# An edge-gated graph layer on one core: the term beta1 h comes from the transposed h by TensorE in blocks 0 to 9, and for half of each later block

## The chip, the cores and the metric

The kernel runs on one core of a Trainium2 chip. The metric is the device time of one execution in microseconds. Before the change the median of three runs is 1077.57 us (1075.32 to 1079.38).

## What is computed

The input x has 16 graphs (b) of 1024 nodes (u, v) with 256 features (d); the adjacency adj is 1024 x 1024 and sparse. Cut to what matters, with A = adj:

```python
pre_u = einsum('bud,dk->buk', h, W1[:256])
pre_v = einsum('bvd,dk->bvk', h, W1[256:])
hidden = relu(pre_u[:, :, None, :] + pre_v[:, None, :, :] + b1)
S = sigmoid(einsum('buvk,ko->buvo', hidden, W2)[..., 0] + b2[0])
a = einsum('buv,bud->bvd', S * A, h)
m = einsum('uv,bud->bvd', A, h) * h
z = beta1 * h + beta2 * (a @ Wa + ba) + beta3 * (m @ Wm + bm)
```

The change concerns the first term of the last line, beta1 * h. All of it is in fp32.

## The kernel before, in words

**Blocks and steps.** A block is a group g of 4 graphs and a tile vt of 128 target nodes v; there are 4 x 8 = 32 blocks (`order`, L409). A block has T = 10 steps: two windows of 64 targets, five tiles of 128 edges each. The loop at L882 runs over n, the 320 steps and a few more; k is the block and s the step in it. In a step, GpSimd gathers 128 rows of a table in DRAM, [pre_u | h] of the source nodes for four graphs (`fetch`, L515, eight buffers `fetched`). TensorE spreads pre_v to the edges (`expand`, L610, into PSUM tile pc), VectorE adds pc to the gathered rows (`add`, L646) and makes the scores by relu, product with W2 and sum (`gate`, L650, four L656). ScalarE takes the sigmoid and builds the left operands (L625, L659, L661). TensorE sums the rows of h into the targets (`aggregate`, L664).

**A window's end and a block's end.** `half_end` (L678) copies the sums out, `turn_over` (L683) transposes them by TensorE (L691) into LT, and `times_h` (L702) multiplies the m half by the transposed h, hT. `block_end` (L710) is a generator that is run for block k - 1 in the steps z to z + 3 of block k, one quarter in each, with z = 4 from n = 10 on. It works in two halves h of two graphs. For each, TensorE puts the bias into PSUM (L719, L449) and adds the products with Wa and Wm (L722), eight matmuls of 256 columns. Then beta1 h is added to it:

- In every block but those of the last group's second half, ScalarE copies the PSUM tile to LT (L736), and one step later VectorE computes h beta1 + z in the tile h_blk (L737). Two steps later the store is issued on SP's queue (L739).
- In the second half of the blocks of the last group (24 to 30), TensorE adds be1_eye times h_blk (L726, two matmuls of 256 columns; be1_eye is the identity times beta1), ScalarE copies PSUM to h_blk (L728), and L730 stores it.

Block 31 has an ending of its own (`tail`, L753).

**Loads of h and of hT.** h_blk, 256 KB for a half, has four buffers and is loaded from the table on SP's queue in steps 5 and 7 of its own block (L916 to L922). hT, 512 KB for a block, is loaded by `load_hT` (L428), on SP's queue but for one; it is read by `rows` (L452, pre_u of a coming group, with w_u), by `halves` (L473, pre_v of the next block, with w_v) and by `times_h`, which after its last use gives the buffer back (`drop_hT`, L706). When hT is loaded and when `rows` uses it is a table written out by hand: `plan` (L787 to L798) gives for each tile the step of the load and of its two pieces. In groups 2 and 3 the load stands at first - 4 + 10 i and the pieces at first + 8 + 10 i and first + 12 + 10 i.

**The order on the engines** is the order in which the program issues (a manual schedule); `after(step, f)` puts f at the end of a later step. In steps up to 110 VectorE, TensorE and GpSimd also make the edge lists (`lists`, L242), in pieces that `fill` (L640) puts between the four L656 of a step. One of their tiles is few (L330), an 8-bit copy that GpSimd writes and four DMAs read. be1_eye is made at step 110 (L942); the other scalings with beta are made in `scale_late` (L599), at step 10.

Of the kernel before, what the change touches and what calls it, by code (L numbers as in the profile page):

```python
# [7 lines left out]
FP = mybir.dt.float32  # L8
# [3 lines left out]
ALU = mybir.AluOpType  # L12
AX = mybir.AxisListType
P = 128
# [3 lines left out]
def kernel(  # L18
# [42 lines left out]
    nc = tc.nc  # L61
    B, N, D = x.shape
    NT = N // P
    DC = D // P
    GB = 4
    NG = B // GB
    GD = GB * D
    W = 64
    NW = P // W
    TW = 5  # L70
    E = TW * P
# [170 lines left out]
    def lists(vt):  # L242
# [84 lines left out]
        nc.vector.tensor_tensor(thr[:, vt:vt + 1], last, none, ALU.add)  # L327
        yield "op"
        RR = lst.tile([P, NW, RC], FP, name="RR", bufs=2)
        few = lst.tile([P, E], mybir.dt.uint8, name="few", bufs=2)  # L330
        yield "slot"
        for w, mine in enumerate((soon, late)):
            nc.vector.tensor_scalar(RR[:, w, :], R, mine, None, ALU.mult)
# [68 lines left out]
    def after(step, f):  # L402
        due.setdefault(step, []).append(f)
# [19 lines left out]
    def drop_hT(k):  # L423
        del hTs[k]
        if k in hT_of:
            hT_free.append(hT_of.pop(k))
# [77 lines left out]
            pass  # L504

    T = TW * NW

    BS = NG * NT

# [89 lines left out]
    def scale_late():  # L599
        nc.vector.tensor_scalar(ba_b, ba_b, be2, None, ALU.mult)  # L600
        nc.vector.scalar_tensor_tensor(bias, bias, be3, ba_b, ALU.mult, ALU.add)
        spread(bias_p, bias)
        nc.vector.tensor_scalar(w_a, w_a, be2, None, ALU.mult)
        nc.vector.tensor_scalar(w_m, w_m, be3, None, ALU.mult)
        hT_free.append(spare_)

# [19 lines left out]

    running = []
    be1_eye = []  # L630

    def piece_of(r, n):

# [49 lines left out]
    def turn_over(k, w, q, step):  # L683
        if w == 0 and q == 0:
            LTs[k] = one.tile([P, GB, 2, DC, P], FP, name="LT")
        LT = LTs[k]
        pt = small("pt").rearrange("p (r k c v) -> p r k c v", r=2, c=DC, v=V)
        ev = evs.pop(q)
        for i in range(4):
            r, c = divmod(i, DC)  # L690
            nc.tensor.transpose(pt[:, r, :, c, :], ev[:, r, c * P:(c + 1) * P], ident)  # L691
        v = slice(w * W + q * U, w * W + (q + 1) * U)
        r = (w * W + q * U) // V
        nc.scalar.copy(LT.rearrange("p b k c (r v) -> p r (b k c) v", v=V)[:, r:r + 2],
                       pt.rearrange("p r k c v -> p r (k c) v"))
        apart = k == BS - 1 and w == NW - 1
        if not apart:
            if not q:
                return
            v = slice(w * W, (w + 1) * W)  # L700

        def times_h():  # L702
            m = LT.rearrange("p (b two) k c n -> p b (two k c) n", two=2)[:, :, DC:3 * DC, v]
            h = hTs[order[k]].rearrange("p (b two) c n -> p b (two c) n", two=2)[:, :, :, v]
            nc.vector.tensor_tensor(m, m, h, ALU.mult)  # L705
            if w == NW - 1 and q == 1:  # L706
                drop_hT(order[k])
        after(step + (1 if k == BS - 1 or w else 2), times_h)

    def block_end(k):  # L710

        g, vt = order[k]
        hb = hbs[k]
        for h in range(2):
            for i, wt in ((1, w_a), (0, w_m)):
                step = yield
                if i:
                    pz = small("pz")
                    add_row(pz, bias_p)  # L719
                for bb in range(2):  # L720
                    for c in range(DC):
                        nc.tensor.matmul(pz[:, bb * D:(bb + 1) * D], LTs[k][:, 2 * h + bb, i if bb else 1 - i, c, :], wt[:, c, :],  # L722
                                         start=False, stop=(i == 0 and c == DC - 1), skip_group_check=True)
            if h == 1 and g == NG - 1:
                for bb in range(2):
                    nc.tensor.matmul(pz[:, bb * D:(bb + 1) * D], be1_eye[0], hb[h][:, bb, :], start=False, stop=True,  # L726
                                     skip_group_check=True)
                nc.scalar.copy(hb[h], pz.rearrange("p (b d) -> p b d", b=2))  # L728
                b = g * GB + 2 * h
                after(step + 2, lambda hb=hb[h], b=b: nc.sync.dma_start(  # L730
                    out[b:b + 2, vt * P:(vt + 1) * P, :].rearrange("b p d -> p b d"), hb))
                continue
            z = pz.rearrange("p (b d) -> p b d", b=2)
            if step >= ROOM:
                z = LTs[k][:, 2 * h].rearrange("p k c n -> p (k c n)").rearrange("p (b d) -> p b d", b=2)
                nc.scalar.copy(z, pz.rearrange("p (b d) -> p b d", b=2))  # L736
            after(step + 1, lambda hb=hb[h], z=z: nc.vector.scalar_tensor_tensor(hb, hb, be1, z, ALU.mult, ALU.add))  # L737
            b = g * GB + 2 * h
            after(step + 2, lambda hb=hb[h], b=b: nc.sync.dma_start(  # L739
                out[b:b + 2, vt * P:(vt + 1) * P, :].rearrange("b p d -> p b d"), hb))  # L740
        del hbs[k], LTs[k]

# [42 lines left out]
    def plan(blocks, ns):  # L787

        for k, (load, *pieces) in zip(blocks, ns):
            loads[load] = k  # L790
            at.update((n, k) for n in pieces)

    plan(turn[NT:], ((1, 2, 4), (2, 8, 9), (5, 12, 18), (10, 19, 22), (20, 28, 29), (23, 32, 38), (30, 39, 42), (40, 48, 49)))
    for g, first in ((2, 60), (3, 140)):
        plan([(g, vt) for vt in range(NT)], ((first - 4 + 10 * i, first + 8 + 10 * i, first + 12 + 10 * i)
                                             for i in range(NT)))
    plan([(1, vt) for vt in range(FIRST)], [(37 + 10 * i,) for i in range(FIRST)])
    plan([(g, vt) for g in range(2) for vt in range(FIRST, NT)], ((103,), (113,), (125,), (133,)))  # L798
    begun = set(turn[:NT])
    end = parts = piece = last = None  # L800
# [81 lines left out]
    for n in range(total + 2):  # L882
        k, s = divmod(n, T)
        if n < total - 3:
            last_in = n - 1 if n % 2 or n < ROOM else done
        else:
            last_in = n
        while done < min(last_in, total):
            gather_in(done)
            done += 1  # L890
        if n % TW == 1 and n // TW + 1 < total // TW:
            load_mark(n // TW + 1)
        if n < LAST:
            expand(n + 2)
            if n >= ROOM:
                fill(n, False)
            products(n, k, s)
        if n + 1 < total:
            add(n + 1)
        if n < total:  # L900
            gate(n)
            if n + 1 < total:
                left_adj(n + 1)
        do(n)
        if s == 8 and ROOM <= n < LAST:
            turn_over(k, 0, 0, n)
        if n >= LAST and n + 2 < total:
            expand(n + 2)
        if n == 1:
            bias = load_rows(bm, D, "bias", nc.sync, spare[:, 1])  # L910
            ba_b = load_rows(ba, D, "ba_b", nc.sync, spare[:, 2])
            be1 = load_rows(beta1, 1, "be1", nc.sync)
            be2 = load_rows(beta2, 1, "be2", nc.sync)
            be3 = load_rows(beta3, 1, "be3", nc.sync)
            after(10, scale_late)
        if s in (5, 7) and k < BS - 1:  # L916
            h = s // 7
            hb = big.tile([P, 2, D], FP, name="h_blk", bufs=4)
            hbs.setdefault(k, []).append(hb)
            g, vt = order[k]  # L920
            nc.sync.dma_start(hb.rearrange("p b d -> p (b d)"),
                              table[g][vt * P:(vt + 1) * P, GD + 2 * h * D:GD + (2 * h + 2) * D])  # L922
        if n == total - 6:
            hbs[BS - 1] = hT_free.pop(0).rearrange("p b c n -> p b (c n)")
            for v, m, f in tails:
                for h, o in tail_rows(x, v, m, f):
                    nc.sync.dma_start(h, o)
        for i in advance.get(n, ()):
            next(made[i], None)
        if n in start_list:  # L930
            running.append([made[start_list[n]], True, n])
            piece_of(running[-1], n)
        if n < ROOM or n >= LAST:
            fill(n, False)
        if n >= LAST:
            products(n, k, s)
        if n == LISTS:
            assert not running and all(next(x, None) is None for x in made)
            lists_done()
            more = main.enter_context(tc.tile_pool(name="more", bufs=1))  # L940
            hT_free.extend(hT_places(more, MORE, NH))
            be1_eye.append(more.tile([P, P], FP, name="be1_eye"))  # L942
            nc.vector.tensor_scalar(be1_eye[0], ident, be1, None, ALU.mult)
        if n == 120:
            nc.gpsimd.partition_all_reduce(longest, rest, P, bass_isa.ReduceOp.max)
            after(n + 12, count_rest)
# [115 lines left out]
```

## Time and profile before

| what | value |
|---|---|
| median of 3 runs | 1077.57 us |
| the profiled execution | 1082.24 us, its span 1080.4 us |
| mean granted TensorE clock | 0.99 |
| DMA | 394.56 MB, mean 365 GB/s |
| gathers (queue 0) | 301.16 MB, 70.9% of the 16 engines' span |
| queue 1 (SP's loads and stores) | 78.66 MB, 22.9% |
| h_blk loads | 62 of 256 KB |
| stores of z from h_blk | 62 of 256 KB |

A page of the profile tells one execution: busy time by engine, the span in 40 slices, the DMA queues, the chain of work that ended last, and the costliest groups of instructions. PE is TensorE, PEld its weight loads, DVE VectorE, ACT ScalarE, POOL GpSimd, SP the engine that only issues DMAs. A group's line gives line number, engine, operation, what it writes and reads (out<-in), its shape and count, busy us and mean ns of one, and the idle time of the engine just before it with what ended it. An fp32 matmul stands in the trace as two records, and the ends of matmuls are modelled, so starts tell more than durations.

### The profile page before, as it was taken

The numbers are of one execution on the slowest core, as the hardware profiler recorded it, in microseconds if no ns is written. First come the engines' busy times: TensorE is split into PE (matmuls) and PEld (weight loads), VectorE is DVE, ScalarE is ACT, GpSimd is POOL, SyncE is SP. The second block draws the span as 40 slices with busy tenths as digits, with TensorE's granted clock in tenths as the row PEclk, the third lists the DMA queues.
The fourth block names the chain that finished last, engine by engine and source line by source line (L and its number), as shares of the span: only waits on it lengthen the run. The fifth ranks groups of instructions, "written<-read, shape, count | busy, mean of one in ns | idle before, by whom it ended". The sixth has DMA issues, their size and how long they took to land.

```text
span 1080.4 us, 24120 instructions
## 1 busy us (share of the span) xinstructions
PE 1020.1 (94%) x7673; PEld 731.3 (68%) x7673; DVE 1017.6 (94%) x3481; ACT 862.6 (80%) x2616; POOL 459.3 (43%) x456
## 2 busy tenths in 40 slices
PE   7777999999999999999999999999999999999996
PEld 6654676776666776677777767777766667666654
DVE  8687999998999999999999999999999999999993
ACT  3246787788888887898888888889889889999983
POOL 2666676555257334553333334333333333333330
PEclk9989999999999999999999999999999999999999
DMA  9999899999999999999999999999999999999991
GB/s 283 327 340 385 313 339 381 362 382 378 403 352 371 408 381 385 379 403 395 404 393 399 412 384 392 408 396 389 381 361 370 369 348 368 365 381 369 365 341 44
DMA packets 147752, 394.56 MB, mean 365 GB/s; under 512 B 18224, under 2 KB 94512, under 8 KB 111408
## 3 DMA queue, kind: packets, MB, share of 16 engines
q0 software_dynamic: 50544, 301.16, 70.9%
q1 hardware_dynamic: 83776, 78.66, 22.9%
q10 hardware_dynamic: 13296, 13.11, 3.5%
q8 instruction: 63, 1.03, 0.4%
q14 instruction: 73, 0.60, 0.1%
HBM read 396.93 MB, written 50.33 MB: 414 GB/s over the span
## 4 chain that ended last, share of the span: by engine, by line
PE 40%; DVE 34%; issue 10%; ACT 8%; DMA 5%; POOL 2%; another core or an unknown queue 0%; POOLq 0%; DVEq 0%; ACTq 0%
DVE fetched L656 16%; DVE fetched L648 12%; PE acc L673 10%; PE misc L722 10%; PE misc L445 9%; PE pc L615 7%; DMA fetched<-table,uidx 3%; PE misc L691 2%; ACT left L661 2%; DVE LT L705 1%; ACT X L489 1%; PE misc L449 1%; DVE low L484 1%; DVE h_blk L737 1%; DMA hT__635<-in_xT_dram 1%
## 5 line engine op out<-in xcount | busy, mean ns | idle before, releaser
L518 POOL DMA_INDIRECT fetched<-table,uidx x320 | 339.4, 1061 | 529.0 <-PE acc L673 389.0
L656 DVE SCALAR_TENSOR_TENSOR fetched<-fetched,w_b 128x256 f32<-128x256 f32 x1280 | 478.0, 419 | 0.0
L648 DVE TENSOR_TENSOR fetched<-fetched,pc 128x1024 f32<-128x1024 f32 x320 | 387.7, 1212 | 29.9 <-PE pc L615 19.4
L661 ACT ACTIVATE left<-left,gt 128x32 f32<-128x32 f32 (+1 forms) x1280 | 299.6, 305 | 10.4
L673 PE MATMUL acc<-fetched,left 128*32 128x256 f32 x4096 | 273.4, 385 | 6.3 <-ACT gt L659 3.7
L615 PE MATMUL pc<-X,mark 128*128 128x512 f32 x640 | 243.7, 462 | 10.9 <-DVE fetched L648 9.3
L673 PEld LDWEIGHTS acc<-fetched,left 128*32 128x32 f32 x4096 | 127.6, 109 | 112.1 <-issue 29.1
L615 PEld LDWEIGHTS pc<-X,mark 128*128 128x128 f32 x640 | 105.4, 189 | 88.9 <-issue 41.6
L659 ACT ACTIVATE gt<-sc,b_b 128x4 f32<-128x4 f32 x320 | 95.9, 300 | 46.7 <-DVE fetched L656 37.5
L722 PE MATMUL misc<-w_m,LT 128*128 128x256 f32 x496 | 117.3, 379 | 0.0
L722 PE MATMUL misc<-w_a,LT 128*128 128x256 f32 x496 | 117.2, 379 | 0.0
L445 PE MATMUL misc<-w_v,hT 128*128 128x256 f32 x448 | 107.6, 383 | 0.0
L722 PEld LDWEIGHTS misc<-w_a,LT 128*128 128x128 f32 x496 | 93.8, 189 | 15.3 <-issue 0.4
L722 PEld LDWEIGHTS misc<-w_m,LT 128*128 128x128 f32 x496 | 93.8, 190 | 15.1
L625 ACT ACTIVATE left<-onehot,val 128x64 f32<-128x64 bf16 (+1 forms) x320 | 102.9, 322 | 0.0
L385 POOL DMA_INDIRECT val<-in_adjT_dram,vidx x80 | 87.2, 1090 | 34.4 <-issue 20.4
L656 DVE DVE_READ_ACCUMULATOR fetched<-fetched,w_b 128x1 f32 x1280 | 100.7, 79 | 0.0
L691 PE MATMUL misc<-ident,ev 128*128 128x128 f32 x512 | 79.5, 278 | 18.5 <-issue 7.0
L445 PEld LDWEIGHTS misc<-w_v,hT 128*128 128x128 f32 x448 | 86.4, 193 | 14.3
L691 PEld LDWEIGHTS misc<-ident,ev 128*128 128x128 f32 x512 | 60.7, 141 | 45.7 <-ACT ev L681 15.2
L482 ACT CAST X<-misc 128x512 fp32r<-128x512 f32 x64 | 37.1, 580 | 55.2 <-PE misc L445 48.0
L445 PE MATMUL misc<-w_u,hT 128*128 128x256 f32 x320 | 76.6, 386 | 4.0 <-issue 3.8
(185 smaller groups left out, 1011.3 us busy)
## 6 DMA issues: line engine op xcount, KB each, us to landing
h_blk<-table SPq DMA_DIRECT2D x62, 256.0 KB
out_dram<-h_blk SPq DMA_DIRECT2D x62, 256.0 KB
hT<-in_xT_dram SPq DMA_DIRECT2D x28, 512.0 KB
table<-in_x_dram ACTq DMA_DIRECT2D x24, 512.0 KB
table<-tab SPq DMA_DIRECT2D x48, 256.0 KB
fetched<-table,uidx POOLq DMA_INDIRECT x320
table<-in_x_dram SPq DMA_DIRECT2D x8, 512.0 KB
table<-fetched SPq DMA_DIRECT2D x8, 512.0 KB
```

Of the source, the lines that this page charges most:

```text
L385: nc.gpsimd.indirect_dma_start(out=val[:, i, j:j + 1], out_offset=None, in_=adj_flat, in_offset=bass.IndirectOffsetOnAxis(ap=vidx[:, i, j: ...
L445: nc.tensor.matmul(p[:, bb * D:(bb + 1) * D], hT[:, 2 * h + bb, i, :], wt[:, i, :], start=(i == 0 and not begun), stop=(i == DC - 1), skip ...
L518: nc.gpsimd.indirect_dma_start(out=fetched[at_slot[n]], out_offset=None, in_=table[g], in_offset=bass.IndirectOffsetOnAxis(ap=uidx[:, vt * ...
L615: nc.tensor.matmul(pcs[n][:, c], marks[n // TW][:, j * P:(j + 1) * P], cuts[k][:, w, c], start=True, stop=True)
L625: nc.scalar.activation(lefts[n][:, :m, 1::GB, :], onehot[:, i, o:o + m, :].unsqueeze(2).to_broadcast([P, m, GB // 2, V]), AF.Copy, scale=v ...
L648: nc.vector.tensor_tensor(t, t, pcs.pop(n), ALU.add)
L656: nc.vector.scalar_tensor_tensor(t[:, b, :], t[:, b, :], 0.0, w2_b, ALU.max, ALU.mult, accum_out=sc[:, b:b + 1])
L659: nc.scalar.activation(gt, sc, AF.Sigmoid, bias=b2_b)
L661: nc.scalar.activation(lefts[n][:, :m, 2 * b, :], lefts[n][:, :m, 1 + b // 2 * GB, :], AF.Copy, scale=gt[:, b:b + 1])
L673: nc.tensor.matmul(accs[h][b * 2 * V:(b + 1) * 2 * V, r, :], left[:, i, 2 * b - b % 2:2 * b - b % 2 + 2].rearrange("p k v -> p (k v)"), f[ ...
L691: nc.tensor.transpose(pt[:, r, :, c, :], ev[:, r, c * P:(c + 1) * P], ident)
L722: nc.tensor.matmul(pz[:, bb * D:(bb + 1) * D], LTs[k][:, 2 * h + bb, i if bb else 1 - i, c, :], wt[:, c, :], start=False, stop=(i == 0 and ...
```

## The change

A function `from_hT(k, h)` says which halves take the new way: both of blocks 0 to 9, the second (h = 1) of blocks 10 to 30. For these, `block_end` adds to PSUM, for each of two graphs and each of two chunks of 128 features, the matmul of hT (as the stationary operand) with be1_eye (128 moving columns). ScalarE copies PSUM into a fresh h_blk tile and SP stores it. No L737 is run and no h is loaded for them. hT is kept until the last of these matmuls has been issued, so `drop_hT` moves from `times_h` to `block_end`, and the loads of hT that follow in the plan are put two steps later, with the pieces where they were. be1_eye becomes a constant tile made in `scale_late`, and few has one buffer in place of two.

```diff
-        few = lst.tile([P, E], mybir.dt.uint8, name="few", bufs=2)
+        few = lst.tile([P, E], mybir.dt.uint8, name="few", bufs=1)
...
+    BOTH, SECOND = range(10), range(10, 31)
...
         hT_free.append(spare_)
+        be1_eye.append(const.tile([P, P], FP, name="be1_eye"))
+        nc.vector.tensor_scalar(be1_eye[0], ident, be1, None, ALU.mult)
...
+    def from_hT(k, h):
+        return k in BOTH or h == 1 and k in SECOND
...
-            if w == NW - 1 and q == 1:
+            if w == NW - 1 and q == 1 and not from_hT(k, 1):
                 drop_hT(order[k])
...
-            if h == 1 and g == NG - 1:
+            if from_hT(k, h):
                 for bb in range(2):
-                    nc.tensor.matmul(pz[:, bb * D:(bb + 1) * D], be1_eye[0], hb[h][:, bb, :], start=False, stop=True,
-                                     skip_group_check=True)
-                nc.scalar.copy(hb[h], pz.rearrange("p (b d) -> p b d", b=2))
+                    for c in range(DC):
+                        nc.tensor.matmul(pz[:, bb * D + c * P:bb * D + (c + 1) * P], hTs[order[k]][:, 2 * h + bb, c, :], be1_eye[0],
+                                         start=False, stop=True, skip_group_check=True)
+                if h == 1:
+                    drop_hT(order[k])
+                hb = big.tile([P, 2, D], FP, name="h_blk", bufs=4)
+                nc.scalar.copy(hb, pz.rearrange("p (b d) -> p b d", b=2))
                 b = g * GB + 2 * h
-                after(step + 2, lambda hb=hb[h], b=b: nc.sync.dma_start(
+                after(step + 2, lambda hb=hb, b=b: nc.sync.dma_start(
...
-        plan([(g, vt) for vt in range(NT)], ((first - 4 + 10 * i, first + 8 + 10 * i, first + 12 + 10 * i)
+        plan([(g, vt) for vt in range(NT)], ((first - 2 + 10 * i, first + 8 + 10 * i, first + 12 + 10 * i)
                                              for i in range(NT)))
-    plan([(1, vt) for vt in range(FIRST)], [(37 + 10 * i,) for i in range(FIRST)])
+    plan([(1, vt) for vt in range(FIRST)], [(39 + 10 * i,) for i in range(FIRST)])
...
-        if s in (5, 7) and k < BS - 1:
+        if s in (5, 7) and k < BS - 1 and not from_hT(k, s // 7):
...
-            be1_eye.append(more.tile([P, P], FP, name="be1_eye"))
-            nc.vector.tensor_scalar(be1_eye[0], ident, be1, None, ALU.mult)
```

## The prediction, made before the changed kernel was run

> **What bounds the kernel now.** I read the page first, then busy time by stretch, then the timeline of one block, the waits and the chain by stretch. The page does not choose between two engines:
>
> ```profile
> PE 1020.1 (94%) x7673; PEld 731.3 (68%) x7673; DVE 1017.6 (94%) x3481; ACT 862.6 (80%) x2616; POOL 459.3 (43%) x456
> DMA  9999899999999999999999999999999999999991
> ```
>
> PE and DVE are level at 94%, and the DMA row is full. The stretches separate them. A line holds the length, busy us and instructions of PE, PEld, DVE, ACT, POOL, the clock, the DMA share and GB/s:
>
> ```profile
> 147.00:187.00 40.00, 39.26 (x295) 28.61 (x288) 40.00 (x144) 32.65 (x100) 25.95 (x27) 1.00 1.03 386
> 250.00:315.00 65.00, 60.34 (x461) 41.93 (x459) 64.10 (x229) 53.08 (x164) 25.83 (x28) 1.00 1.01 379
> 684.00:744.00 60.00, 59.86 (x464) 43.46 (x463) 57.58 (x191) 52.40 (x162) 21.57 (x20) 1.00 1.02 402
> 863.00:948.00 85.00, 82.54 (x655) 58.26 (x654) 85.00 (x283) 76.69 (x237) 30.13 (x30) 1.00 0.95 357
> ```
>
> From 863 us on DVE has no idle time and PE has some: DVE sets the pace, 28.2 us a block. From 442 to 804 us PE is idle for 0.1 us in 30 and DVE for 1.2: PE sets it, 30.1 us a block. A busy PE can still be a stretched one, so I looked at the starts (start, us, engine, line):
>
> ```profile
> 697.63 1.89 PE L445 MATMUL misc<-w_v,hT 128*128 128x256 f32 x8
> 699.17 0.82 PE L615 MATMUL pc<-X,mark 128*128 128x512 f32 x2
> 699.82 0.40 PE L449 MATMUL misc<-bias_p,unit 128*128 128x512 f32 x1
> 700.05 1.89 PE L722 MATMUL misc<-w_a,LT 128*128 128x256 f32 x8
> 687.08 1.22 DVE L648 TENSOR_TENSOR fetched<-fetched,pc 128x1024 f32<-128x1024 f32 x1 [1.20 <-PE pc L615]
> DVE fetched L648 <- PE pc L615: 12.2, 13, 1.2
> ```
>
> Eight L722 follow each other at (1.89 - 0.379)/7 = 0.216 us, the next group starts where they stop, and no PE row of this block carries an idle mark. The last two lines are DVE's: once a block it waits 1.2 us for PE (the second sums this over 500 to 804 us). So PE is full there and DVE has 1.2 us of room. Before 442 us the pace changes hands. The chain over 190 to 250 us lies mainly on PE, over 250 to 315 us on DVE:
>
> ```profile
> by line: PE misc L445 21.7%; PE acc L673 21.5%; PE misc L722 17.3%; PE pc L615 14.3%; PE misc L691 5.8%; ACT left L661 4.1%; ACT X L489 3.5%; PE misc L449 2.3%; issue 2.1%; ACT LT L736 2.0%; ACT gt L659 1.4%; ACT left L625 1.2%; ACT mark L5
> by line: DVE fetched L656 32.7%; DVE fetched L648 30.1%; issue 13.0%; DVE h_blk L737 3.2%; DVE LT L705 2.8%; DVE cand L261 2.4%; DVE low L484 2.3%; PE misc L691 1.9%; DVE key L252 1.9%; DVE made L322 1.2%; PE pc L615 0.7%; DVE made L315 0.7
> ```
>
> The same view gives PE for 107 to 250 and 315 to 378 us and DVE for most of 378 to 442.
>
> **What the Trainium skill says.** "TensorE: Matmul & The Clock Gate", section "LDWEIGHTS (loading the stationary operand)": a weight load takes as many ns as it has columns, over 1.2, so 107 for 128. The trace has no bare load, but ten 58-column matmuls with a 128-column load each (L341) start (1.22 - 0.275)/9 = 0.105 us apart, which agrees. The same page, "Step-by-step: what each phase is for": the next load runs beside the running matmul. L722 agrees: loads of 0.19 us do not show in 0.216. "FP8 and Floating Point Precision", "TensorE Precision Notes": true fp32 takes four passes; the trace shows two records a matmul (28 of L726 for 14 in the code). "DMA: Bandwidth & Descriptors", "Issuing engines are not separate DMA queues": all queues share 16 engines, so a dropped load helps gathers too.
>
> ```profile
> L737 DVE SCALAR_TENSOR_TENSOR h_blk<-h_blk,be,LT 128x512 f32<-128x512 f32 x55 | 40.9, 744 | 0.0
> L726 PE MATMUL misc<-h_blk,be_eye 128*128 128x256 f32 x28 | 7.2, 379 | 0.0
> L341 PE MATMUL misc<-RR,made 128*128 128x58 f32 x50 | 6.1, 269 | 0.0
> ```
>
> **The change, part by part.** *Off DVE:* L737 goes for 20 halves in blocks 0 to 9 and 14 in blocks 10 to 23 (21 more stay). The next instruction starts 0.66 us after it (707.12 to 707.78), so 34 x 0.66 = 22.4 us leave DVE.
>
> *On PE:* four matmuls a half, two records each, 128 moving columns. From below: half of L722's 0.216, 0.108; L341 says loads allow 0.105; four transposes of L691 (0.60 us, the last 0.27) start 0.11 apart. From above, nothing overlapped: load 0.107 plus stream 0.108, 0.216. I take 0.11, because L722 hides its loads: 0.88 us a half, 1.76 a block up to 9, 0.88 in 10 to 23. In blocks 24 to 30, 8 x 0.11 replace 4 x 0.216: nothing.
>
> *ACT:* L736's copy (582 ns) becomes L728's (566): nothing, hidden or not. It waits for 0.88 us more of PE; behind it queue gate and X casts, so ACT passes PE's lateness on, already in PE's price. Its buffer must be free of a store issued some 18 steps earlier (four buffers, two halves a block); the longest wait for a landed store on SP's queue was 18.8 us, 18 steps are over 50. Nothing.
>
> *DMA:* 41 of 62 loads of 256 KB go, 10.7 of 394.6 MB. Gathers delay an add visibly only at 103 to 107 us (4.3 us, put to a queue). Worth 0 to 1.4 us there (two loads, 0.52 MB at 0.38 MB/us); I take 0.7. Elsewhere they hide behind PE and DVE.
>
> *Moved loads of hT:* two steps later, after the freeing matmuls. In SP's queue each is moved past the dropped load and the first store, which waits for ACT's copy. From 12 steps to first use 10 remain, about 30 us. In the trace's packets the three loads issued at 523, 556 and 586 us landed 26 to 29 us later, 6 to 9 us ahead of use: a cover of 0 to 3 us is left, less what the lighter queue returns. Nothing; if it fails, up to 3 us each for three loads. *be1_eye earlier, one buffer of few:* a DVE op of 0.2 us in block 1; POOL's casts come over 10 us apart, and the earlier DMAs had landed. Nothing.
>
> *The sum,* on the profiled execution (1082.24 us; span 1080.4). A block's end is executed in the next block.
> - 107 to 250 us, ends of blocks 0 to 3, PE on the chain: 4 x 1.76 = 7.0; PE waits there of about 3 us can swallow part: **+4.0** (0.5 to 7).
> - 250 to 315, ends 4 and 5, DVE on the chain: -4 x 0.66 = -2.6; PE's 4.7 us idle takes the 3.5 added: **-2.0** (-2.6 to +1).
> - 315 to 378, ends 6 and 7, PE: +3.5, 0.6 idle: **+2.5** (0 to 3.5).
> - 378 to 442, ends 8 and 9: DVE -2.6, but PE is idle for 2.0 against 3.5 added, so PE is late next: **0** (-1.5 to +1.5).
> - 442 to 804, ends 10 to 21, PE: 12 x 0.88 = 10.6, less a wait in block 11: **+10.0** (8 to 10.6). DVE's saved 0.66 only lengthens its wait for PE.
> - 804 to 862, ends 22 and 23: DVE -1.3, PE idle 1.7 for 1.8: **-0.3** (-1.3 to +0.5). After that nothing.
>
> With the 0.7 for DMA, +13.5 us: 1095.7 profiled. That execution lay 4.7 us above the median of 1077.57, so **1091 us**. The lower ends together give +2 (1079), the upper +24 (1102); loads not overlapped at all would double PE's price.
>
> **Rivals.** (a) *The transfers set the pace* (faster). Place: blocks 1 to 22, where the DMA share is 1.00 to 1.03. Price: 0.52 MB a block at 0.38 MB/us, 1.38 us in blocks 0 to 9, 0.67 in 10 to 23: 10 x 1.38 + 14 x 0.67 = 23 us, 1055; with half, 1066. It decides from the point where an add or a matmul waits for a gather. For it: the full DMA row. Against: over 500 to 804 us DVE's waits name PE, and PE has no gap for a transfer to sit in. (b) *The early blocks pay it back* (no change). DVE's 13.3 us of blocks 0 to 9 come off in full while PE's waits swallow 17.6: -10 against +10, 1078. For it: DVE's idle time is near 0 at 147 to 187 us. Against: PE's idle time is as small there. (c) *Loads show, or hT comes late* (slower still): 0.216 a record in the PE stretches adds some 20 us, 1111.
>
> **Chances.** Mine 0.70 (own range 1080 to 1101), (a) 0.10, (b) 0.12, (c) 0.08. 0.5%, 5.4 us, is about what a measurement here can tell from no change: faster is (a); same is (b) with the low edge of mine, 0.15; slower 0.75. The range drops (a) and half of (c): 1075 to 1104.
>
> **What would show it.** Right: a block of 684 to 744 us takes 31.0 instead of 30.1 us, DVE's wait for pc grows to about 2.7 us a block, the new records start 0.11 us apart. Wrong: those blocks keep 30.1 us or fall; records 0.2 us apart; PE rows that wait for hT; blocks 1 to 10 shorter by over 8 us in all.

## The result and the profile after

The changed kernel takes 1088.14 us (median of 4 runs, 1085.63 to 1088.48) against 1078.25 us (4 runs, 1075.32 to 1079.38) of the kernel before: ratio 1.0091, 95% interval 1.0065 to 1.0117. It is slower by 9.9 us; 1091 was forecast. The two profiled executions lie at opposite ends: that of before (1082.24 us) is slower than all four of its timed runs, that of after (1085.63 us, span 1083.8) is the fastest of its four. So the traces differ by 3.4 us in all, and only their parts can be compared.

On the page, TensorE rises from 1020.1 to 1040.4 us of busy time, VectorE falls from 1017.6 to 998.2. The DMA row stays as full as it was:

```profile
PE 1040.4 (96%) x7973; PEld 761.8 (70%) x7973; DVE 998.2 (92%) x3447; ACT 860.7 (79%) x2616; POOL 452.7 (42%) x456
DMA  9999999999999999999999999999999999999981
```

The four stretches that the prediction showed, in the same columns:

```profile
147.00:187.00 40.00, 38.62 (x302) 28.61 (x301) 37.96 (x144) 30.88 (x93) 24.85 (x26) 1.00 1.00 365
250.00:315.00 65.00, 63.87 (x497) 46.36 (x497) 64.43 (x236) 53.95 (x165) 24.96 (x26) 1.00 1.00 365
684.00:744.00 60.00, 59.86 (x472) 43.79 (x471) 55.01 (x184) 50.63 (x160) 20.29 (x20) 1.00 1.01 375
863.00:948.00 85.00, 83.22 (x677) 59.71 (x676) 85.00 (x284) 77.31 (x241) 30.89 (x30) 1.00 0.96 352
```

In the third, PE's busy time is the same 59.86 us as before. A full engine can't get busier: what changes is how much of the kernel it gets through, and DVE, which follows it, falls from 57.58 to 55.01 us and from 191 instructions to 184. In the second, PE goes from 60.34 to 63.87 us and its lines shown here make up 45% of the chain, on which it had next to nothing before (2.6% in the lines shown):

```profile
by line: DVE fetched L662 12.4%; PE acc L679 11.6%; PE misc L728 10.7%; PE misc L445 9.3%; DVE fetched L654 8.8%; PE pc L618 7.2%; ACT left L667 5.7%; issue 5.1%; PE misc L697 3.1%; PE misc L733 2.8%; ACT LT L700 2.4%; DVE cand L261 2.3%; A
```

The new matmuls in the timeline of one block (start, us, engine, line), and the add that follows:

```profile
710.06 1.89 PE L728 MATMUL misc<-w_m,LT 128*128 128x256 f32 x8
711.78 1.05 PE L733 MATMUL misc<-be_eye,hT 128*128 128x128 f32 x8
712.59 0.71 PE L618 MATMUL pc<-X,mark 128*128 128x512 f32 x2
...
686.97 1.22 DVE L654 TENSOR_TENSOR fetched<-fetched,pc 128x1024 f32<-128x1024 f32 x1 [2.08 <-PE pc L618]
```

(1.05 - 0.275)/7 = 0.111 us from start to start, and L618 begins 0.81 us after the first of them. The 41 halves have 328 such records, of which the trace holds 296. By groups and by waits (us in total, times, longest; 500 to 804 us, where it was 12.2 before):

```profile
L733 PE MATMUL misc<-be_eye,hT 128*128 128x128 f32 x296 | 39.0, 275 | 0.0
L747 DVE SCALAR_TENSOR_TENSOR h_blk<-h_blk,be,LT 128x512 f32<-128x512 f32 x21 | 15.6, 741 | 0.0
```

```profile
DVE fetched L654 <- PE pc L618: 23.9, 18, 2.1
```

A block's start can be read in the timeline as the start of its first add. From the differences (us; the second execution of before comes from the experiments below, the kernel being the same):

| part | before | before, second | after | what runs there |
|---|---|---|---|---|
| up to block 0 | 66.3 | 61.1 | 62.1 | start |
| block 0 | 34.3 | 36.8 | 36.1 | |
| blocks 1 to 4 | 143.0 | 137.4 | 139.9 | ends 0 to 3 |
| blocks 5, 6 | 69.5 | 68.3 | 67.3 | ends 4, 5 |
| blocks 7, 8 | 59.4 | 59.0 | 61.8 | ends 6, 7 |
| blocks 9, 10 | 68.7 | 67.1 | 68.1 | ends 8, 9 |
| block 11 | 30.3 | 29.2 | 29.8 | end 10 |
| blocks 12 to 22 | 332.5 | 337.3 | 341.3 | ends 11 to 21 |
| blocks 23, 24 | 58.6 | 58.8 | 58.2 | ends 22, 23 |
| blocks 25 to 30 | 169.2 | 169.3 | 169.2 | |
| block 31 and tail | 48.7 | 49.0 | 50.0 | |

Two places show the change cleanly: in blocks 12 to 22 the usual block takes 31.0 us for 30.1 (the second trace of before has 7 us more in block 14, of which later), and block 24 takes 28.2 for 28.9, since DVE's operation of block 23's second half is gone. The first three rows show how far two executions of one kernel lie apart: 8.2 us at the start of block 5. Much of that may be the chip. Block 2 begins at 133.1 us in the trace of after and at 132.8 to 134.8 in the four traces of the experiments' second set, but at 140.8 in the first trace of before and at 139.5 to 145.6 in the eight traces of the other three sets, each set on a chip of its own. The record does not name the chip of the first two traces; by these starts, it is the second trace of before that compares like with like.

### The profile page after: what moved, and what is told of

The parts are those of the page before. It is cut to its first block, busy times and chain, and to the rows that moved or that the text cites. A ratio compares the mean times of both kernels' runs of the same rounds, so it can differ in the third digit from the quotient of the medians.

```text
span 1083.8 us, 24664 instructions
## 1 busy us (share of the span) xinstructions
PE 1040.4 (96%) x7973; PEld 761.8 (70%) x7973; DVE 998.2 (92%) x3447; ACT 860.7 (79%) x2616; POOL 452.7 (42%) x456
## 4 chain that ended last, share of the span: by engine, by line
PE 55%; DVE 23%; ACT 8%; DMA 7%; issue 4%; SPq 2%; ACTq 0%; POOL 0%; POOLq 0%; DVEq 0%
PE misc L728 14%; PE acc L679 13%; PE misc L445 11%; DVE fetched L662 10%; DVE fetched L654 10%; PE pc L618 9%; ACT left L667 3%; PE misc L697 3%; PE misc L733 3%; DMA table<-in_x_dram 2%; DMA fetched<-table,uidx 2%; PE misc L449 2%; DVE LT L711 1%; DVE low L484 1%; DMA hT__635<-in_xT_dram 1%
## 5 line engine op out<-in xcount | busy, mean ns | idle before, releaser
L519 POOL DMA_INDIRECT fetched<-table,uidx x320 | 333.3, 1042 | 538.4 <-PE acc L679 405.1
L679 PE MATMUL acc<-fetched,left 128*32 128x256 f32 x4096 | 268.5, 384 | 3.4 <-ACT left L667 3.1
L618 PE MATMUL pc<-X,mark 128*128 128x512 f32 x640 | 240.4, 457 | 10.0 <-DVE fetched L654 10.0
L618 PEld LDWEIGHTS pc<-X,mark 128*128 128x128 f32 x640 | 103.1, 191 | 83.6 <-issue 40.9
L445 PE MATMUL misc<-w_v,hT 128*128 128x256 f32 x448 | 107.1, 382 | 0.0
L385 POOL DMA_INDIRECT val<-in_adjT_dram,vidx x80 | 86.1, 1077 | 32.0 <-issue 18.9
L445 PEld LDWEIGHTS misc<-w_v,hT 128*128 128x128 f32 x448 | 86.0, 192 | 14.0
L482 ACT CAST X<-misc 128x512 fp32r<-128x512 f32 x64 | 37.1, 580 | 55.4 <-PE misc L445 55.4
L700 ACT COPY LT<-misc 128x512 f32<-128x512 f32 x128 | 72.9, 570 | 3.3 <-PE misc L697 3.3
## 6 DMA issues: line engine op xcount, KB each, us to landing
h_blk<-table SPq DMA_DIRECT2D x21, 256.0 KB, 10.5
table<-in_x_dram SPq DMA_DIRECT2D x8, 512.0 KB, 10.5
```

Of the source, the lines that this page charges most:

```text
L385: nc.gpsimd.indirect_dma_start(out=val[:, i, j:j + 1], out_offset=None, in_=adj_flat, in_offset=bass.IndirectOffsetOnAxis(ap=vidx[:, i, j: ...
L445: nc.tensor.matmul(p[:, bb * D:(bb + 1) * D], hT[:, 2 * h + bb, i, :], wt[:, i, :], start=(i == 0 and not begun), stop=(i == DC - 1), skip ...
L519: nc.gpsimd.indirect_dma_start(out=fetched[at_slot[n]], out_offset=None, in_=table[g], in_offset=bass.IndirectOffsetOnAxis(ap=uidx[:, vt * ...
L618: nc.tensor.matmul(pcs[n][:, c], marks[n // TW][:, j * P:(j + 1) * P], cuts[k][:, w, c], start=True, stop=True)
L679: nc.tensor.matmul(accs[h][b * 2 * V:(b + 1) * 2 * V, r, :], left[:, i, 2 * b - b % 2:2 * b - b % 2 + 2].rearrange("p k v -> p (k v)"), f[ ...
```

## The experiments

The runs fall in four sets on different chips, whose kernel before took 1087.28, 1076.98, 1083.65 and 1082.94 us (medians of 35, 40, 41 and 11 runs). Each ratio is to before in its own set; it is not the quotient of the two medians, from which it differs by up to 0.0022.

**The middle blocks back to VectorE.** TensorE's way is kept in blocks 0 to 9 and in the second halves of 24 to 30; the later loads of hT stay.

```diff
-    BOTH, SECOND = range(10), range(10, 31)
+    BOTH, SECOND = range(10), range(24, 31)
```

> The changed kernel with SECOND = range(24, 31): the second halves of blocks 10 to 23 go back to the load of h and the VectorE operation. Theory (TensorE sets the pace in blocks 12 to 22, each half there costs 0.9 us): the ratio to the kernel before falls from 1.009 to 0.998 to 1.002, about 1078 us, and a block between 684 and 744 us takes 30.1 us again. Rival (the early blocks or the later loads of hT cost the time): the ratio stays at 1.006 or more.

Measured: 1103.66 us, 1.0141 (1.0118 to 1.0164). The middle blocks did fall to 30.1 us, but some did not (31.4 in block 12, 31.8 in 15, 32.6 in 21), and block 12 began only at 487.1 us. The theory's interval is missed and the rival's (1.006 or more) met. Beside the trace of the dropped loads alone (below, on the same chip), block 12 begins 9.9 us later and blocks 12 to 22 take 3.7 us more. So something else in the change costs, most of it before block 12, which the full change hides or which these loads of h bring back. The next sets look for it.

**The early blocks back to VectorE.**

```diff
-    BOTH, SECOND = range(10), range(10, 31)
+    BOTH, SECOND = (), range(10, 31)
```

> The changed kernel with BOTH empty: blocks 0 to 9 go back to the load of h and the VectorE operation, the second halves of 10 to 30 stay on TensorE. Theory as I hold it after the result (early blocks about even, all of the loss in 10 to 23): ratio 1.007 to 1.011, about 1088 us. As the prediction's sum had it (early blocks cost about 4 us): 1.004 to 1.006. Rival (early blocks pay back): above 1.012.

Measured: 1097.09 us, 1.0092 (1.0063 to 1.0120). Blocks 12 to 22 take 31.1 us. One half a block on TensorE, where it is full, is enough for a loss as large as the whole, and larger than the 1.004 to 1.006 that the prediction's sum gave. (The later loads of hT stay in this kernel, beside the loads of h of blocks 0 to 9; no matmul after 98 us of its trace waits for one.)

**The new matmuls left out.** The eight records of each half are not issued (41 halves of z are without beta1 h); all else of the change stays.

```diff
-                for bb in range(2):
-                    for c in range(DC):
-                        nc.tensor.matmul(pz[:, bb * D + c * P:bb * D + (c + 1) * P], hTs[order[k]][:, 2 * h + bb, c, :], be1_eye[0],
-                                         start=False, stop=True, skip_group_check=True)
```

> The changed kernel without the matmuls of hT with be1_eye: beta1 h is left out of z in the 41 halves that take the new way; all else (copies, stores, dropped loads, later loads of hT) as changed. Theory (the loss is the records' own time on TensorE): blocks 12 to 22 take 30.1 us again and the early blocks keep VectorE's saving, 1062 to 1074 us, ratio 0.985 to 0.996. Rival (the later release of hT, the copy's waits or the order of SP's queue cost the time): ratio 1.005 or more.

Measured: 1083.14 us, 0.9954 (0.9933 to 0.9976). Blocks 12 to 22 are at 30.2 us again. The matmuls are the loss; all that the change takes away is worth 0.5% with nothing paid for it, some 5 us of the 22.4 that leave VectorE.

**The loads dropped, nothing else.** In the kernel before, VectorE keeps beta1 h everywhere, but for the 34 halves that the change takes from it, it reads w_m in place of h (z has w_m in place of h there) and no h is loaded.

```diff
+            of_h = w_m if unloaded(k, h) else hb[h]
...
-            after(step + 1, lambda hb=hb[h], z=z: nc.vector.scalar_tensor_tensor(hb, hb, be1, z, ALU.mult, ALU.add))
+            after(step + 1, lambda to=to, of_h=of_h, z=z: nc.vector.scalar_tensor_tensor(to, of_h, be1, z, ALU.mult, ALU.add))
...
-        if s in (5, 7) and k < BS - 1:
+        if s in (5, 7) and k < BS - 1 and not unloaded(k, s // 7):
```

> The kernel before with 34 of the 62 loads of h dropped (blocks 0 to 9 both halves, 10 to 23 the second) and nothing else changed: VectorE's operation reads a constant tile (w_m) in place of h, so beta1 h is not in z there. Theory (transfers are covered): 1076 to 1078 us, ratio 0.997 to 1.001. Rival (the DMA engines set the pace): 8.9 MB less at 0.38 MB/us, up to 23 us, ratio 0.98 to 0.99.

Measured: 1086.69 us, 0.9996 (0.9978 to 1.0014). Dropping 8.9 MB does nothing by itself, although the DMA row is full from end to end. The transfers don't set the pace.

**The two kernels again, in the second set.**

> The changed kernel itself, beside the kernel before, in one session with the runs below. The two earlier parts do not add up: blocks 0 to 9 back alone left 1.0092, 10 to 23 back alone gave 1.0141, yet both together were first measured at 1.0091. Theory A (the parts add): 1.022 to 1.026 wherever the kernel before takes 1087 us, with blocks 0 to 11 some 10 us later than before, and about 1.009 where it takes 1078 us. Theory B (dropping the loads of 10 to 23 returns what the early blocks lose): 1.008 to 1.012 here too.

> The kernel before, unchanged: 0.997 to 1.003. It is run for a second trace, to see how much blocks 0 to 3, where the first gathers, copies and hT loads crowd the DMA engines, differ from run to run: 2 to 8 us from the first trace by block 4, under 1 us from block 12 on.

Measured: the changed kernel 1087.85 us, 1.0117 (1.0077 to 1.0157); the kernel before 1077.24, 1.0008 (0.9985 to 1.0030). The base of this set was 1077, so it can't tell an effect of the chip. The second trace of before was worth more: from block 12 on it should have followed the first within 1 us, but block 14 takes 37.1 us. Its timeline there (in brackets: idle us, and what ended it) and the stretches (length, busy us of PE, PEld, DVE, ACT, POOL, granted clock, DMA share, GB/s):

```profile
525.47 0.40 PE L449 MATMUL misc<-b_p,unit 128*128 128x512 f32 x1
529.98 3.78 PE L445 MATMUL misc<-w_v,hT 128*128 128x256 f32 x8 [4.11 <-DMA hT<-in_xT_dram]
```

```profile
525.00:530.00 5.00, 0.89 (x4) 0.41 (x4) 5.00 (x19) 2.42 (x8) 1.78 (x2) 0.84 1.03 420
530.00:533.00 3.00, 3.00 (x7) 2.46 (x8) 0.04 (x2) 0.00 (x0) 0.00 (x0) 0.50 0.95 389
533.00:536.00 3.00, 3.00 (x10) 2.37 (x10) 1.34 (x2) 2.17 (x8) 0.00 (x0) 0.62 0.94 346
```

A load of hT is late, PE stands for 4.1 us, and then its eight L445 take 3.78 us in place of 1.89, at half the clock: 7 us from one late load, in the kernel before with its own plan of loads. That is the Trainium skill's "TensorE: Matmul & The Clock Gate", section "What's actually happening": after an idle window of some 3.4 us the array gets half its pulses until it has been busy for at least as long. The trace agrees on the half, with 0.50 granted; how long the window is it does not show.

**TensorE's way only where VectorE sets the pace.**

```diff
-    BOTH, SECOND = range(10), range(10, 31)
+    BOTH, SECOND = (4, 5, 8, 9), range(23, 31)
```

> The changed kernel with BOTH = (4, 5, 8, 9) and SECOND = range(23, 31): TensorE takes beta1 h only where VectorE lay on the chain. Theory (the pace-setting engine decides, stage by stage): 3 to 4 us faster than before, ratio 0.996 to 0.999. Rival (every half on TensorE costs, by a longer PSUM hold or the later release of hT): 1.002 to 1.005.

Measured: 1082.69 us, 1.0075 (1.0053 to 1.0096). In its trace, beside the second one of before, the blocks meant did get shorter (5: 33.5 for 34.7; 6: 32.4 for 33.6; 9: 32.1 for 33.9; 24: 28.2 for 29.1; block 10 did not, 33.8 for 33.2). The ratio is outside both intervals: what was gained there was lost elsewhere. Block 13 takes 40.7 us, block 3 39.2, block 8 32.7. In block 3 PE waits 4.5 us for ACT's copy into a table tile; in block 13 it is hT again:

```profile
PE misc L445 <- DMA hT<-in_xT_dram: 6.1, 1, 6.1
```

**The matmuls twice** from block 10 on (beta1 h is then counted twice in 21 halves).

```diff
-                for bb in range(2):
+                for bb in list(range(2)) * (2 if k >= 10 else 1):
```

> The changed kernel with the matmuls of hT with be1_eye issued twice in blocks 10 to 30, so that beta1 h is counted twice in z there. Theory (TensorE is full in blocks 12 to 22): a block between 684 and 744 us goes from 31.05 to 31.9 us, and in blocks 25 to 30, where TensorE had some 0.7 us of room, from 28.2 to 28.2 to 28.6; 9 to 13 us above the changed kernel in all. Rival (the loss is a fixed cost of the new way, not the records' time): within 2 us of the changed kernel.

Measured: 1100.66 us, 1.0233 (1.0192 to 1.0274), 12.8 us above the changed kernel of the same set. Blocks 12 to 22 take 31.9 us, blocks 25 to 30 28.3 to 28.4. The doubled group in the timeline:

```profile
689.37 1.95 PE L733 MATMUL misc<-be_eye,hT 128*128 128x128 f32 x16
```

(1.95 - 0.275)/15 = 0.112 us a record. 0.9 us more a block where PE is full; next to nothing where DVE is.

**The later loads of hT alone.**

```diff
-        plan([(g, vt) for vt in range(NT)], ((first - 4 + 10 * i, first + 8 + 10 * i, first + 12 + 10 * i)
+        plan([(g, vt) for vt in range(NT)], ((first - 2 + 10 * i, first + 8 + 10 * i, first + 12 + 10 * i)
...
-    plan([(1, vt) for vt in range(FIRST)], [(37 + 10 * i,) for i in range(FIRST)])
+    plan([(1, vt) for vt in range(FIRST)], [(39 + 10 * i,) for i in range(FIRST)])
```

> The kernel before with one edit: the loads of hT of groups 1 (first half), 2 and 3 stand two steps later, as in the change; all 62 loads of h stay and VectorE does beta1 h everywhere. Theory: the later loads fit only when the loads of h are dropped; under the full traffic a load of hT takes 20 to 29 us against some 30 us of lead that are left, so w_v's matmuls (L445) of one to four blocks wait 2 to 7 us for hT; ratio to before 1.003 to 1.010, and blocks without such a wait keep 30.1 us. Rival: the stalls of the two mixed versions came from elsewhere (their mix of ways, the order of the stores), the later loads cost nothing as the prediction said; ratio 0.998 to 1.002 and no more waits for hT than the kernel before has.

Measured: 1091.73 us, 1.0071 (1.0044 to 1.0097). The profiled execution (1106.46 us) was the slowest of twelve and is not counted in the ratio, so it shows what can happen, not how often, and not what the other eleven lose. Its timeline and stretches in block 13:

```profile
497.18 0.43 SPq L434 DMA_DIRECT2D hT<-in_xT_dram  x1
...
531.88 3.78 PE L445 MATMUL misc<-w_v,hT 128*128 128x256 f32 x8 [8.43 <-DMA hT<-in_xT_dram]
535.10 1.37 PE L615 MATMUL pc<-X,mark 128*128 128x512 f32 x2
536.31 1.89 PE L445 MATMUL misc<-w_u,hT 128*128 128x256 f32 x8
```

```profile
520.00:531.80 11.80, 3.13 (x31) 1.76 (x31) 7.42 (x31) 4.96 (x17) 1.97 (x2) 0.76 1.02 399
531.80:536.00 4.20, 4.12 (x10) 3.32 (x11) 0.00 (x0) 0.30 (x1) 0.00 (x0) 0.50 0.90 285
```

The load was issued at 497.18 us; w_v's matmuls waited 8.4 us for it, began at 531.88 us, 34.7 us after the issue, and ran at half the clock. DVE and ACT stand with it, and the block takes 41.5 us. Late hT is not the only stall here: in block 9 (38.4 us) PE waits 4.2 us for ACT's copy into a table tile, and ACT waits 5.4 us for a store of the table to land. Since the second trace of before has one wait for hT too, it is the ratio, and not the count of waits, that speaks against the rival.

How long a load takes to land is counted here, and in the prediction, from queue 1's packets of 512 B in the order of their start, 1024 to a load. The trace does not say to which load a packet belongs, so these times are estimates, and may be short: for this load the count gives 528.0 us, 3.9 us before the matmuls could begin.

**The later loads and the dropped loads together**: the kernel before with that plan and with the 34 dropped loads (w_m in place of h in those halves, as above).

> The same later loads of hT, and the 34 loads of h that the change drops from VectorE's halves are dropped too: there VectorE multiplies w_m in place of h (so z has w_m in place of h in these halves), with its time unchanged. Theory: with the lighter queue the later loads are in time, hT lands in 12 to 15 us, no matmul waits for it; ratio 0.998 to 1.001, below that of the later loads alone by 0.003 or more. Rival: the later loads cost nothing in either, and the two ratios lie within 0.002 of each other.

Measured: 1083.98 us, 1.0000 (0.9979 to 1.0020), 0.0071 below the later loads alone, in the same set. No matmul waits for a load of hT in flight in its blocks 1 to 30. By the count of packets, its loads issued between 580 and 730 us took 11 to 20 us to land; in the changed kernel it is 12 to 14, in the first trace of before 21 to 29, in the kernel with the later loads alone 18 to 25.

**Only what the end of the kernel can use.** TensorE's way in the second halves of blocks 23 to 30, loads of hT where they were before.

```diff
-    BOTH, SECOND = range(10), range(10, 31)
+    BOTH, SECOND = (), range(23, 31)
...
-        plan([(g, vt) for vt in range(NT)], ((first - 2 + 10 * i, first + 8 + 10 * i, first + 12 + 10 * i)
+        plan([(g, vt) for vt in range(NT)], ((first - 4 + 10 * i, first + 8 + 10 * i, first + 12 + 10 * i)
...
-    plan([(1, vt) for vt in range(FIRST)], [(39 + 10 * i,) for i in range(FIRST)])
+    plan([(1, vt) for vt in range(FIRST)], [(37 + 10 * i,) for i in range(FIRST)])
```

> The changed kernel with BOTH empty and SECOND only blocks 23 to 30, loads of hT where they stood before: TensorE takes one more half than before (block 23) and in blocks 24 to 30 reads hT in place of a loaded h_blk. Theory: block 24 gets 0.7 us shorter (29.1 to 28.3), blocks 25 to 30 keep 28.2 us, everything before block 23 is as before: -0.7 us, ratio 0.998 to 1.000. Rival: the eight matmuls of 128 columns with a load each do cost time where VectorE sets the pace, or hT that is given back later delays a load of the last group: blocks 25 to 30 over 28.5 us and a ratio over 1.002.

Measured: 1083.35 us, 0.9996 (0.9978 to 1.0015). Block 24 takes 28.2 us, blocks 25 to 30 28.2, blocks 12 to 22 30.1. The 0.7 us of block 24 are in the trace; the time can't tell them from nothing. This version equals the kernel before, no more.

**The early blocks alone.** The changed kernel without the matmuls of the second halves of blocks 10 to 23 (z is without beta1 h in those 14).

```diff
-                for bb in range(2):
+                for bb in range(0 if 10 <= k < 24 else 2):
```

> The changed kernel without the new matmuls of the second halves of blocks 10 to 23 (so beta1 h is left out of z in these 14 halves); everything else of the change stays: TensorE's way in blocks 0 to 9, the dropped loads, the later loads of hT. So blocks 12 to 22 should take 30.1 us again, block 24 about 28.2, and what is left is the net of the change in blocks 0 to 9. Theory (the prediction's stretches): +4.0 - 2.0 + 2.5 + 0 up to 442 us, -0.7 for the start, -1 from blocks 23 and 24: about +3, ratio 1.001 to 1.005. Rival 1, the early blocks pay back (VectorE's 13 us count in full): ratio 0.990 to 0.998. Rival 2, TensorE's 17.6 us in the early blocks show in full: ratio 1.008 to 1.012, and the middle blocks were then not the main loss.

Measured: 1093.60 us, 1.0097 (1.0063 to 1.0131), outside what the theory gave and inside the second rival's interval. The middle is back (30.2 us in blocks 12 to 22, 28.2 in block 24), so on this chip the early blocks alone cost 10.5 us. Blocks 2 to 11 by stretch, in the columns of above: the second trace of before, the changed kernel in the same set, then this kernel:

```profile
134.20:458.90 324.70, 315.67 (x2402) 228.46 (x2404) 321.86 (x1122) 270.22 (x822) 174.09 (x169) 1.00 1.03 386
132.80:464.90 332.10, 328.40 (x2543) 244.71 (x2543) 311.15 (x1103) 269.01 (x821) 168.17 (x170) 1.00 1.00 362
140.80:480.30 339.50, 332.58 (x2535) 245.17 (x2534) 311.54 (x1100) 270.61 (x822) 168.00 (x170) 1.00 0.99 356
```

The first two are of one chip. There the stretch gets 7.4 us longer, PE's idle time falls from 9.0 us to 3.7, and DVE's grows from 2.8 to 21. So the early blocks have the middle's fault: VectorE's relief of 11 us is all idle time, because TensorE has become the full engine there too. A part of what divides the second line from the third is the chip's. Up to the end of block 9 the two kernels issue the same instructions, and yet block 12 begins at 464.9 us in one and at 480.3 in the other; of these 15.4 us, 8.0 are there when block 2 begins. The kernel before takes 6.0 us more in this set than in the second (1082.94 for 1076.98), so that much would be in the ratio's base too. In block 1 PE waits once for ACT's copy into a table tile, as it does not in the traces of the changed kernel:

```profile
PE misc L445 <- ACT tab L461: 7.4, 1, 7.4
```

## Why the prediction was right, point by point

**What bounds the kernel.** Right. PE is full from 503 to 804 us: eight more records a block make it 0.9 us longer, sixteen 1.8 (30.1, 31.0, 31.9), and dropped loads change nothing.

**The price.** 0.11 us a record was taken between 0.108 and 0.216; 0.111 and 0.112 were measured. The 107 ns for a load of 128 columns, an estimate from the rule in the Trainium skill ("TensorE: Matmul & The Clock Gate", "LDWEIGHTS (loading the stationary operand)"), comes close, and so does half of the 256-column matmul; which of the two is the limit no run tells.

**The middle.** +10.0 (8 to 10.6) was summed for ends 10 to 21. The rows give -0.5 + 8.8 = +8.3: 0.80 us a block for the 0.88 of PE's work, and block 11 with no loss. Against the second trace they give +0.6 + 4.0, and 7.0 more without its stalled block 14. (The prediction's "idle for 0.1 us in 30" holds from 503 us on; from 442 to 503 PE was idle for 2.0, the room in block 11.) The early-back version gives the same by the clock, 1.0092. DVE's saved operation became a longer wait: 23.9 us from 500 to 804 us for 12.2. Over its 18 waits and ten blocks that is 2.4 us a block where 2.7 was named.

**Ends 22 and 23**: -0.3 was said, -0.4 measured. **Blocks 25 to 30**: nothing was said and 0.0 measured; the doubled kernel shows that there was room.

**The early stretches.** Against the first trace, ends 4 and 5 give -2.2 (-2.0 said), ends 6 and 7 +2.4 (+2.5), ends 8 and 9 -0.6 (0). Ends 0 to 3 give -3.1 where +4.0 was summed; block 4 alone has +3.8 (30.9 to 34.7), but block 1 -5.3, since the stall of 4.3 us that before had at 103 us is not there. The second trace of before has no such stall in block 1 (36.2 us for 40.2); against it the four are +2.5, -1.0, +2.8 and +1.0, in sum +5.3 for +4.5.

**The start and the loads of h**: -0.7 us was read from one execution, and no run bears it out or refutes it: by themselves the dropped loads are worth 0.9996 (0.9978 to 1.0014). Up to block 1's end the first trace of before and that of after differ by 7.7 us, of which the second trace of before has 6.6 without any change.

**The total**: +13.5 us was summed and 9.9 measured, and the total came nearer (1091 for 1088) than the parts allow. The 4.7 us by which the profiled execution lay above the median were taken for chance; by the start of block 2 they may belong to another chip. Between the two traces of one chip, in the second set, the parts are +5.7 (blocks 1 to 10), +0.5 (block 11), +3.9 (12 to 22) and -0.1 (the rest). The +3.9 would be +10.9 without the 7.0 us that before loses in block 14 to late hT; the two traces of the changed kernel have no such stall. That before loses some us in this way now and then, and the changed kernel with its lighter queue does not, would close the gap, but how often it happens was not measured. To that extent the nearness is luck.

**The loads of hT, two steps later**: "Nothing" was said, with a cover of 0 to 3 us "less what the lighter queue returns", and 3 us each if it fails. For the changed kernel nothing is right, but only because the loads of h are gone: with them the same plan costs 0.71% (0.44 to 0.97), without them 0.00% (-0.21 to 0.20). The price of a failure was too low: one late load cost 7.0 us in the second trace of before (4.1 of waiting), 10.6 in the second mixed version (6.1) and 11 in the later loads alone (8.4), a part of the rest being matmuls at half the clock. The cover of 0 to 3 us rested on a count of packets that was 3.9 us short in the one load shown. Late hT is seen in the second of the two mixed versions, which bring back loads of h and keep the later plan (1.0075). In the trace of the first (1.0141) there is one wait for hT, of 1.4 us; most of its loss lies in the early blocks, which it keeps on TensorE. The skill's sentence used in the prediction ("DMA: Bandwidth & Descriptors", "Issuing engines are not separate DMA queues"), that all queues share the 16 engines, is not tested by this pair of kernels: the dropped loads stand on the same queue of SP as the loads of hT.

**The rivals.** The transfers as the bound: refuted by the dropped loads alone. Early blocks that pay back: refuted by the early blocks alone, 1.0097. Loads that show: refuted by 0.111 us. Late hT: in no trace of the changed kernel does a matmul wait for it after 98 us.

**What stays open.** The middle alone (1.0092) and the early blocks alone (1.0097) together are more than the whole (1.0091 and 1.0117). They ran on different chips, and the same early program took 15 us more up to block 12 on one of them, 6 of which the kernel before takes more there too. Without any of the new matmuls the ratio was 0.9954, with those of the early blocks 1.0097, on yet another pair of chips: 15.5 us for 17.6 of PE's work, which would leave little for PE's waits to swallow. So the net of the early blocks is some +5 us, as summed and as the second trace of before and that of after give it, or about twice that; a comparison of the early-only and the whole kernel on one chip was not made. Nor was the tail looked into: block 31 and what follows take 50.0 and 49.5 us in the two traces of the changed kernel and 48.7 to 49.7 in kernels with the loop of before, though of the change only block 30's end runs there; two kernels that have the same end but no block of the first ten on TensorE take 48.7 and 48.5.

## What to carry to other kernels

Work moved from one engine to another is worth what the receiver has idle in that stretch: here PE had 0.1 us in 30 and paid in full, while most of DVE's 34 saved operations became idle time. Read start-to-start times of the receiver, not the page's 94% against 94%. A load that is put later to suit a buffer is to be tried with the rest of the queue as it will be, since its cover depends on what else is loaded.

## What was not expected of the hardware

- A stop of TensorE cost its length and some 3 us more in two cases: after 4.1 and 8.4 us without work the granted clock was 0.50, eight matmuls took 3.78 us for 1.89, and the blocks were 7.0 and 11 us longer. Late data cost more than the wait shows.
- A 512 KB load of hT took from 6 us (by the count of packets) to 34.7 us (until its matmuls could begin) within one execution (the later loads alone, 400 to 800 us); its lead has to be chosen for the slowest and not for the mean.
- The kernel before took 1077 to 1087 us in the four sets, each on its own chip, and whatever the kernel, block 2 began at 133 to 135 us on one of these chips and at 140 to 146 on the others. That is as large as the effects looked for here, so a trace of before and one of after are to be taken on one chip.
